# First message layer of a two-layer graph network: the steps of the last four chunks drawn together, with gathers up to three chunks ahead

## The chip, the cores and the metric

One core of one Trainium2 chip runs the whole kernel in one launch. The metric is the device time of an execution in microseconds (us); lower is better. The engines are PE (TensorE), DVE (VectorE), ACT (ScalarE), POOL (GpSimd, which here issues the indirect gathers) and SP (SyncE, which issues the plain DMAs).

## The reference

The graph has 12,500 nodes of 128 features and 400,000 edges, sorted by destination. Two layers are computed, each on the normalized and rectified nodes `h = relu(layernorm(x))`:

```
# layer 0, per edge:
h   = relu([h[src], h[dst], edge_attr] @ We1 + be1)      # 32 wide
em  = relu(h @ We2 + be2)                                # 128 wide
h2  = relu([h[dst], em] @ Wn1 + bn1)                     # 64 wide
nm  = relu(h2 @ Wn2 + bn2)                               # 128 wide
x  += h + segment_sum(nm, dst)
# layer 1, per edge, with 8 relations:
H   = einsum('ni,rio->rno', relu(layernorm(x)), W)
x  += relu(segment_sum((H[type, src] + b[type]) * weight, dst))
```

## The kernel before, in words

Layer 0 works on 391 chunks of 1,024 edges (`NC` = 391, `CT` = 8 tiles of 128 edges; the last chunk has the number L = 390). Three chunks make a span, whose destinations lie in one window of 128 nodes; there are 131 spans. One chunk passes through these steps, each a method of `Edges` (line numbers of the kernel before):

- `gathered` (L765, by `gather_a`, L426): eight indirect gathers issued by POOL (L394), two to one tile `gb`, which fetch the source's 32-wide product from `tab_a`.
- `turned` (L472): four DVE transposes of `gb` (L477) into `agT`. Each waits for its two gathers to land.
- `end_T` (L453, DVE): one-hot of the destinations for the window's products.
- `first` (L467, L469, PE into the bank `pre`), `first_src` (L485, DVE, twice, into `z`), `first_end` (L489, ACT).
- `second` (L496 PE into `pm0`, `pm1`; L501 ACT, twice).
- `third` (L507, L510 PE into `u`; L513 ACT).
- `fourth` (L520, PE into `pq0`, `pq1`), `fourth_sum` (L528 DVE and L529 ACT, twice each), `fourth_end` (L534 DVE, twice); the last two together are `valued`.
- `ends` (L539, DVE): one-hot `oh` of the destinations, two buffers.
- `sum_up` (L755, by `fifth`, L548 PE): eight matmuls that add the chunk into the span's bank `acc`; the span's last chunk also brings in the row carried from the span before (L554).

When a span is complete, `Span.end` (L749) and `rows_h` (L600) turn its 128 sums into rows of layer 1: a reduction of `acc` (L559), a normalization (L604, L579, L581, L583 on ACT, L588, L590), a transpose (L612 on PE, L614 on ACT), two products of 512 columns (L619) with their additions (L620), and a store into `tab_h` (L621). They are drawn in pieces, one at each `node_step`; `Span.deviate` and `Span.begin` prepare the window's own nodes (L579 to L583, and L588, L590, L596). The PSUM banks `pre`, `pm0`, `pm1`, `u`, `pq0`, `pq1` and `acc` exist once each.

The order of SP, DVE, ACT and PE is the order in which the program draws the instructions: `in_order` ties each to the one drawn before it on its engine. The loop at L801 is a software pipeline written by hand. Turn i draws `first` of chunk i, `second` and `third` of chunk i-1, `fourth` and `valued` of chunk i-2, `sum_up` of chunk i-3, the gathers of chunk i+1 and their four transposes, spread over the turn. So a chunk takes four turns, and three turns without a new chunk follow chunk L. In `gather_a`, `past` says which earlier chunk's transposes a gather must wait for ("not too far ahead"): near the end that is the chunk just before.

Layer 1 starts when all of `tab_h` is stored. Its POOL queue holds 3,128 gathers (L394 too, into `hg`), which DVE multiplies and reduces and PE adds up.

Of the kernel before, what the change touches and what calls it, by code (L numbers as in the profile page):

```python
# [31 lines left out]
CT = 8  # L32
CE = CT * P
SC = 3
ST = SC * CT
NT = -(-E // P)
NC = -(-E // CE)
NS = -(-NC // SC)
# [5 lines left out]
GT = 2  # L44
# [10 lines left out]
def gnn_kernel(  # L55
# [43 lines left out]
    def in_order(start, *engines):  # L99

        for i in block.bb.instructions[start:]:
            if i.engine in engines:
                if i.engine in queues:
                    tc.add_manual_dep(
                        i, queues[i.engine].name,
                        mybir.DependencyInfo(mybir.DependencyClass.NoSync,
                                             mybir.DependencyReason.DATA), reason="in order")
                queues[i.engine] = i
# [62 lines left out]
    def from_byte(table, first, n, most):  # L171

        row = in_bytes(table)
        width = row.shape[1]
        first = nc.s_assert_within(
            first, 0, most * width, skip_runtime_bounds_check_because="a least dst is a node")
        return row.rearrange("n d -> (n d)")[ds(first, n * width)].rearrange("(n d) -> n d", n=n)
# [12 lines left out]
    with tc.tile_pool(name="n0", bufs=2) as pool, \  # L190
# [18 lines left out]
        def products():  # L209

            i, q, m, hT = quads.pop(0)
            (acb, rs), (g, n) = acbs[i], groups[i]
            pn = psum.tile([P, 4, P], F32, name="pn")
            for j in range(m):
                nc.tensor.matmul(pn[:, j, :], hT[:, j, :], w_node, start=True, stop=True)
            if i > len(groups) // 2 and q % 8:
                nc.vector.tensor_copy(acb[:, q:q + m, :], pn[:, :m, :])
            else:
                nc.scalar.copy(acb[:, q:q + m, :], pn[:, :m, :])
            if q + m == n:  # L220
                at = pool.tile([P, GJ, 32], F32, name="at")
                nc.vector.tensor_tensor(at[:, :n, :], acb[:, :, 0:32],
                                        rs[:, :, None].to_broadcast([P, n, 32]), op=OP.mult)
                nc.sync.dma_start(a_g[:, g:g + n, :], at[:, :n, :])

        def turned(i):
            n = groups[i][1]
            for q in range(0, n, 4):
                m = min(4, n - q)
                pt = psum.tile([P, 4, P], F32, name="pt")  # L230
                for j in range(m):
                    nc.tensor.transpose(pt[:, j, :], xms[i][:, q + j, :], ident)
                hT = pool.tile([P, 4, P], F32, name="hT", bufs=4)
                nc.scalar.activation(hT[:, :m, :], pt[:, :m, :], AF.Relu)
                quads.append((i, q, m, hT))
                if len(quads) > 2:
                    products()

        for i, (xg, (g, n)) in enumerate(zip(xs, groups)):
# [4 lines left out]
            k = g - g0  # L244
# [25 lines left out]
            if i >= 3:  # L270
                turned(i - 3)
        for i in range(max(0, len(groups) - 3), len(groups)):
            turned(i)
# [150 lines left out]
    turns = {}  # L424

    def gather_a(idx, c=None):  # L426


        gbs = []
        past = c and c - max(1, 16 - c // 8)  # L430
        for t in range(0, CT, GT):
            gb = gpool.tile([P, GT, 32], F32, name="gb", bufs=16 * CT // GT)
            key = None if c is None else f"gb{c}_{t}"
            gather([gb[:, j, :] for j in range(GT)], tab_a, [idx(t + j) for j in range(GT)], key,
                   turns.get((past, t // GT)))
            gbs.append((gb, key))
        return gbs

    class Edges:
# [25 lines left out]
        def first(self, eat):  # L465
            self.pre = self.psum.tile([64, 512], F32, name="pre")
            nc.tensor.matmul(self.pre, w_ea, eat, start=True, stop=False)  # L467
            for h in range(2):
                nc.tensor.matmul(self.pre[32 * h:32 * h + 32, :], self.win[:, 64:96],  # L469
                                 self.half_T(h), start=False, stop=True)  # L470
# [66 lines left out]
        def ends(self, rel):  # L537
            self.oh = self.pool.tile([P, CT, P], F32R, name="oh", bufs=2)
            nc.vector.tensor_tensor(self.oh, self.iota[:, None, :].to_broadcast([P, CT, P]),  # L539
                                    rel[:, :, None].to_broadcast([P, CT, P]), op=OP.is_equal)  # L540
# [11 lines left out]
    def carry(acc, s, sums):  # L552

        nc.tensor.matmul(acc[0:1, 0:D], carried[:, s:s + 1], sums, start=False, stop=False)  # L554
# [69 lines left out]
    with tc.tile_pool(name="e0", bufs=2) as pool, \  # L624
# [6 lines left out]
        chunks, spans, rows, relbs, eats = {}, {}, {}, {}, {}  # L631
        active = []
        before = [None]

        def node_step():
            if active and next(active[0], "done") == "done":
                active.pop(0)
# [21 lines left out]
        def load(c):  # L659
            if c < NC:  # L660
                chunks[c] = Edges(pool, psum, iota_p, nid_p)
                chunks[c].load_win(from_byte(tab_cb, rows[c // SC][c % SC], WR, 3 * (NP - WB)))
# [92 lines left out]
        def sum_up(c):  # L755
            s, k = divmod(c, SC)
            of = spans[s]
            if k == 0:
                of.acc = psum.tile([P, 2 * D], F32, name="acc")
            stop = k == SC - 1 or c == NC - 1  # L760
            chunks.pop(c).fifth(of.acc, k == 0, stop,
                                (lambda: carry(of.acc, s, before[0])) if stop and s else None)
            return spans.pop(s) if stop else None

        def gathered(c):  # L765
            idx = src0 if c * CT < T0 else src_sb
            return gather_a(lambda t: idx[:, c * CT + t:c * CT + t + 1], c)
# [4 lines left out]
        def valued(c):  # L772
            chunks[c].fourth_sum()
            chunks[c].fourth_end()
# [4 lines left out]
        def end_T(c):  # L779
            chunks[c].ends_T(relbs[c // SC][:, c % SC, :])  # L780
# [12 lines left out]
        gbs = gathered(0)  # L793
# [4 lines left out]


        L = NC - 1  # L800
        for i in range(L + 3):  # L801
            s, k = divmod(i, SC)
            new, two, three = i <= L, 0 < i <= L + 1, 1 < i
            if i < L:
                gbs = gathered(i + 1)

            def turned(q):
                if i < L:
                    turns[i + 1, q] = chunks[i + 1].turned(q, gbs[q])

            if new:
                first(i)
            if k == SC - 1:
                load_eat(s + 2)
            if two:
                chunks[i - 1].second()
            whole = sum_up(i - 3) if i > 2 else None
            if new:
                chunks[i].first_src()
                chunks[i].first_end()  # L820
            turned(0)
            if three:
                chunks[i - 2].fourth()
                ends(i - 2)
            turned(1)
            if i < L:
                end_T(i + 1)
            if k == 1:
                head(s + 2)
                load_relb(s + 2)  # L830
            if k == 0:
                node_step()
            turned(2)
            if three:
                chunks[i - 2].fourth_sum()
            node_step()
            if two:
                chunks[i - 1].third()
            turned(3)
            if three:  # L840
                chunks[i - 2].fourth_end()
            load(i + AHEAD)
            if k == 0:
                if s:
                    spans[s - 1].begin()
                if s not in spans:
                    spans[s] = Span(s)
            if k == 1 and new:
                spans[s].deviate()
            if i == L - 2:  # L850
                for s in range(s + 1, NS):
                    spans[s] = Span(s)
            if i == L - 1:
                for s in range(s + 1, NS):
                    spans[s].deviate()
            if i == L + 1:
                spans[NS - 1].begin()
            if whole:
                active.append(whole.end(["pre"] * 3))
            next(prepared, None)  # L860


        last = sum_up(L)
        node_step()
        steps = last.end(("u", "pm0", "pm1"))
        for k in range(3):
            node_step()
            next(steps)
        for _ in steps:
            pass  # L870
        in_order(start, ENG.SP, ENG.DVE, ENG.Activation, ENG.PE)


# [281 lines left out]
```

## Time and profile before

| | us |
|---|---|
| median of 3 runs (lowest, highest) | 7961.75 (7959.56, 7962.12) |
| profiled execution, its own time | 7943.7 |
| its span in the profile | 7941.9 |
| POOL busy | 5946.7 (75%) |
| DVE busy | 5323.5 (67%) |
| PE busy | 3699.1 (47%) |
| first gather of layer 1 starts at | 4021.04 |

All moments in this document are microseconds from the start of the span. A line of the timeline gives the start, the duration, engine, line, operation, tiles and count, and in brackets the idle time of the engine before it and what ended that. A line of the table by stretches gives for each engine its busy time and, in parentheses, its instructions, then the granted clock of PE (1.00 is full), the DMA share and GB/s.

### The profile page before, as it was taken

Reading aid. Unit: us, or ns where it says so; the run is one execution under the profiler, and the core shown is the slowest. Engines: PE = TensorE matmul, PEld = TensorE weight load, DVE = VectorE, ACT = ScalarE, POOL = GpSimd, SP = SyncE. Lnnn points to the kernel's source line nnn. Section 1 sums busy time; section 2 is a strip of 40 time slices with the busy share of each in tenths; the row PEclk is TensorE's granted clock in tenths of the full one; section 3 lists DMA queues with packets and bytes.
Section 4 is the critical chain, followed back from the end, with each engine's and each line's share of the span. In section 5 each row is a group of like instructions: output and inputs, shape, how many; then the busy total and the mean of one; then the engine's idle time right before and its main releaser. Section 6 shows DMA issues by size and latency. Waiting matters only on the chain. (4 is left out here: it accounts for less than half of the span.)

```text
span 7941.9 us, 54373 instructions
## 1 busy us (share of the span) xinstructions
PE 3699.1 (47%) x13981; PEld 1867.5 (24%) x13982; DVE 5323.5 (67%) x9464; ACT 1691.9 (21%) x3217; POOL 5946.7 (75%) x6273
## 2 busy tenths in 40 slices
PE   4888888888888888888821111111111110111111
PEld 2444444444444444444410000000000000000000
DVE  7978777777777777777755555555555555555555
ACT  3433333333333333333310000000000000000000
POOL 6777777777777777777767777777777777777776
PEclk7988988888888888888855555555555555555555
DMA  5544433333333323333222222222222222222222
GB/s 167 146 99 97 99 91 87 94 87 90 91 88 92 91 87 94 88 90 91 87 56 57 57 57 57 57 57 57 57 57 57 57 57 57 57 57 57 57 57 54
DMA packets 605541, 614.39 MB, mean 77 GB/s; under 512 B 361633, under 2 KB 465893, under 8 KB 604767
## 3 DMA queue, kind: packets, MB, share of 16 engines
q1 hardware_dynamic: 403064, 353.77, 14.3%
q0 software_dynamic: 200192, 256.65, 14.3%
q8 instruction: 115, 1.88, 0.1%
q14 instruction: 206, 1.68, 0.1%
q10 hardware_dynamic: 1964, 0.41, 0.0%
HBM read 509.91 MB, written 100.43 MB: 77 GB/s over the span
## 5 line engine op out<-in xcount | busy, mean ns | idle before, releaser
L394 POOL DMA_INDIRECT hg<-tab_h,hidx_sb x3128 | 2951.3, 944 | 993.3 <-issue 952.6
L394 POOL DMA_INDIRECT gb<-tab_a,src_sb x3032 | 2863.9, 945 | 924.1 <-issue 722.6
L1070 DVE TENSOR_TENSOR v<-hg,io_p 128x1024 f32<-128x1024 f32 x782 | 960.0, 1228 | 1619.2 <-DMA hg<-tab_h,hidx_sb 1610.3
L1040 PE MATMUL acc<-hm,oh 128*128 128x256 f32 x782 | 347.5, 512 | 3514.6 <-DVE oh L1035 3481.5
L1040 PEld LDWEIGHTS acc<-hm,oh 128*128 128x128 f32 x782 | 205.7, 304 | 3675.3 <-issue 3640.4
L1075 DVE TENSOR_REDUCE sm<-v 128x128 f32<-128x1024 f32 x782 | 959.1, 1227 | 9.0
L1078 ACT CAST hm<-sm 128x256 fp32r<-128x256 f32 x391 | 145.5, 372 | 3778.0 <-DVE sm L1075 3778.0
L477 DVE STREAM_TRANSPOSE agT<-gb 128x64 f32<-128x64 f32 x1564 | 376.5, 241 | 734.0 <-DMA gb<-tab_a,src_sb 715.4
L520 PE MATMUL pq<-w_n,h 128*128 128x256 f32 x3128 | 846.7, 420 | 0.0
L529 ACT ACTIVATE nm<-pq 128x512 fp32r<-128x512 f32 x782 | 449.0, 597 | 1339.3 <-DVE pq L528 1338.2
L467 PE MATMUL pre<-eats,w_ea 128*64 128x512 f32 x782 | 473.8, 691 | 481.2 <-DVE ht L620 278.0
L520 PEld LDWEIGHTS pq<-w_n,h 128*128 128x128 f32 x3128 | 647.8, 217 | 89.5 <-issue 0.8
L548 PE MATMUL acc<-nm,oh 128*128 128x256 f32 x3128 | 607.0, 335 | 21.6 <-DVE nm L534 16.7
L548 PEld LDWEIGHTS acc<-nm,oh 128*128 128x128 f32 x3128 | 479.9, 221 | 434.8 <-issue 134.4
L501 ACT ACTIVATE em<-pm,b_e 128x512 f32<-128x512 f32 x782 | 491.0, 678 | 400.8 <-PE pm L496 400.2
L528 DVE TENSOR_TENSOR pq<-pq,b_n 128x512 f32<-128x512 f32 x782 | 505.1, 682 | 58.6 <-PE pq L520 55.9
L496 PE MATMUL pm<-h,w_e 32*128 32x512 f32 x1564 | 526.8, 755 | 0.0
L534 DVE SCALAR_TENSOR_TENSOR nm<-pq,nm 128x512 fp32r<-128x512 f32 x782 | 489.6, 664 | 0.1
L453 DVE TENSOR_TENSOR ohT<-relb,io_p 126x1024 bf16<-126x1024 bf16 x391 | 462.2, 1182 | 6.2 <-DMA relb<-rel_d 6.2
L539 DVE TENSOR_TENSOR oh<-io_p,rel_s 128x1024 fp32r<-128x1024 f32 x391 | 463.3, 1185 | 0.0
L510 PE MATMUL u<-em,w_msg 128*64 128x512 f32 x1564 | 419.8, 616 | 0.2 <-ACT em L501 0.2
L485 DVE TENSOR_TENSOR z<-pre,agT 64x256 f32<-64x256 f32 x782 | 317.3, 406 | 33.0 <-PE pre L469 23.0
(125 smaller groups left out, 3443.5 us busy)
## 6 DMA issues: line engine op xcount, KB each, us to landing
eats<-in_ea SPq DMA_DIRECT2D x131, 768.0 KB
relb<-rel_d SPq DMA_DIRECT2D x131, 756.0 KB
tab_h<-ht SPq DMA_DIRECT2D x131, 576.0 KB
hg<-tab_h,hidx_sb POOLq DMA_INDIRECT x3128
gb<-tab_a,src_sb POOLq DMA_INDIRECT x3032
win<-tab_cb SPq DMA_DIRECT2D x391, 23.6 KB
xw<-tab_h SPq DMA_DIRECT2D x131, 64.0 KB
out<-o SPq DMA_DIRECT2D x131, 64.0 KB
```

What stands on the lines that cost most here:

```text
L394: g = nc.gpsimd.indirect_dma_start(out=out, out_offset=None, in_=table, in_offset=bass.IndirectOffsetOnAxis(ap=idx, axis=0))
L467: nc.tensor.matmul(self.pre, w_ea, eat, start=True, stop=False)
L496: nc.tensor.matmul(pm, w_e2[rows, :], self.h1[rows, :], start=True, stop=True)
L501: nc.scalar.activation(em, pms[h], AF.Relu, bias=b_e2)
L520: nc.tensor.matmul(pq[:, 2 * i:2 * i + 2, :], self.h2[:, P * (2 * k + i):P * (2 * k + i) + P], w_n2, start=True, stop=True)
L528: nc.vector.tensor_add(pq, pq, b_n2[:, None, :].to_broadcast([P, 4, D]))
L534: nc.vector.scalar_tensor_tensor(nm[:, :, 1, :], pq, 0.0, nm[:, :, 0, :], op0=OP.max, op1=OP.subtract)
L539: nc.vector.tensor_tensor(self.oh, self.iota[:, None, :].to_broadcast([P, CT, P]), rel[:, :, None].to_broadcast([P, CT, P]), op=OP.is_equal)
L548: nc.tensor.matmul(acc, self.oh[:, i, :], self.nm[:, at, :, :].rearrange("p q d -> p (q d)"), start=(start and i == 0), stop=(stop and i = ...
L1040: nc.tensor.matmul(acc[:, 0:2 * D], oh[:, q, :], hm[:, q, :, :].rearrange("p r d -> p (r d)"), start=begin and q == 0, stop=stop and q == 1)
L1070: reads(nc.vector.tensor_tensor(v, hg, w_p[:, q, t:t + CT, None].to_broadcast([P, CT, D]), op=OP.mult), f"hg{c}")
L1075: nc.vector.tensor_reduce(sm[:, q, :], v.rearrange("p t d -> p d t"), AX.X, OP.add)
```

## The change

The loop now ends after turn L-4. The last four turns, and what follows, are written out. In them a chunk's steps no longer stand in four different turns: chunks L-4, L-3 and L-2 catch up, chunk L-1 has `first` to `valued` in its own turn, and chunk L too. The four transposes of chunks L-1 and L stand together at the end of the turn before. The instructions are the same ones, in the same number. For chunks above L-5 the gathers wait for the transposes of the chunk three before them.

```diff
-        past = c and c - max(1, 16 - c // 8)
+        past = c and c - (3 if c > NC - 6 else max(1, 16 - c // 8))
...
-        for i in range(L + 3):
+        for i in range(L - 3):
...
+        i = L - 3
+        gbs = gathered(i + 1)
+        first(i)
+        chunks[i - 1].second()
+        sum_up(i - 3)
+        begun(i)
+        turned(i + 1, 0)
+        chunks[i - 2].fourth()
+        ends(i - 2)
+        node_step()
+        turned(i + 1, 1)
+        end_T(i + 1)
+        node_step()
+        chunks[i - 1].third()
+        valued(i - 2)
+        load(L)
+        node_step()
+        spans[s - 2].begin()
+        spans[s - 1] = Span(s - 1)
+        ends(i - 1)
+        chunks[i - 1].fourth()
+        valued(i - 1)
+        node_step()
+        turned(i + 1, 2)
+        turned(i + 1, 3)
+
+        i = L - 2
+        gbs = gathered(i + 1)
+        first(i)
+        chunks[i - 1].second()
+        sum_up(i - 3)
+        whole = sum_up(i - 2)
+        begun(i)
+        ends(i - 1)
+        end_T(i + 1)
+        chunks[i - 1].third()
+        chunks[i].second()
+        chunks[i - 1].fourth()
+        close(whole)
+        chunks[i - 1].fourth_sum()
+        chunks[i].third()
+        chunks[i - 1].fourth_end()
+        node_step()
+        ends(i)
+        chunks[i].fourth()
+        valued(i)
+        spans[s - 1].deviate()
+        spans[s] = Span(s)
+        node_step()
+        all_turned(i + 1)
+
+        i = L - 1
+        gbs = gathered(L)
+        first(i)
+        sum_up(i - 2)
+        sum_up(i - 1)
+        begun(i)
+        node_step()
+        chunks[i].second()
+        end_T(L)
+        ends(i)
+        node_step()
+        chunks[i].third()
+        spans[s - 1].begin()
+        spans[s].deviate()
+        chunks[i].fourth()
+        valued(i)
+        spans[s].begin()
+        all_turned(L)
+
+        first(L)
+        whole = sum_up(L - 1)
+        begun(L)
+        close(whole)
+        chunks[L].second()
+        ends(L)
+        node_step()
+        chunks[L].third()
+        node_step()
+        chunks[L].fourth()
+        node_step()
+        valued(L)
+        node_step()
+        for _ in sum_up(L).end(("u", "pm0", "pm1")):
+            pass
```

Here `begun` is `first_src` and `first_end`, `all_turned` the four transposes, and `close` starts the rows of a complete span; `s` is L / 3 = 130.

More of the change, by code (lines that the diff above doesn't have):

```diff
@@ L800, in gnn_kernel, with turned, begun @@
         L = NC - 1
-        for i in range(L + 3):
-            s, k = divmod(i, SC)
[L803 to L812, printed above, removed]
+        def turned(c, q):
+            turns[c, q] = chunks[c].turned(q, gbs[q])
+        def begun(c):
+            chunks[c].first_src()
+            chunks[c].first_end()
+        for i in range(L - 3):
+            s, k = divmod(i, SC)
+            two, three = 0 < i, 1 < i
+            gbs = gathered(i + 1)
+            first(i)
             if k == SC - 1:
@@ L817, in gnn_kernel @@
             whole = sum_up(i - 3) if i > 2 else None
[L818 to L821, printed above, removed]
+            begun(i)
+            turned(i + 1, 0)
             if three:
@@ L824, in gnn_kernel @@
                 ends(i - 2)
-            turned(1)
-            if i < L:
-                end_T(i + 1)
+            turned(i + 1, 1)
+            end_T(i + 1)
             if k == 1:
@@ L832, in gnn_kernel @@
                 node_step()
-            turned(2)
+            turned(i + 1, 2)
             if three:
@@ L838, in gnn_kernel @@
                 chunks[i - 1].third()
-            turned(3)
+            turned(i + 1, 3)
             if three:
@@ L847, in gnn_kernel @@
                     spans[s] = Span(s)
-            if k == 1 and new:
+            if k == 1:
                 spans[s].deviate()
[L850 to L857, printed above, removed]
             if whole:
@@ L860, in gnn_kernel, with all_turned, close @@
             next(prepared, None)
-        last = sum_up(L)
-        node_step()
[L865 to L869, printed above, removed]
+        def all_turned(c):
+            for q in range(CT // GT):
+                turned(c, q)
+        def close(whole):
+            active.append(whole.end(["pre"] * 3))
+        assert L % SC == 0
+        s = L // SC
+        i = L - 3
+        gbs = gathered(i + 1)
@@ new lines, in gnn_kernel @@
+        first(i)
+        chunks[i - 1].second()
+        sum_up(i - 3)
+        begun(i)
+        turned(i + 1, 0)
+        chunks[i - 2].fourth()
+        ends(i - 2)
+        node_step()
+        turned(i + 1, 1)
+        end_T(i + 1)
[10 more added lines that the diff above has]
+        node_step()
@@ new lines, in gnn_kernel @@
+        turned(i + 1, 2)
+        turned(i + 1, 3)
+        i = L - 2
+        gbs = gathered(i + 1)
+        first(i)
[4 more added lines that the diff above has]
+        ends(i - 1)
+        end_T(i + 1)
+        chunks[i - 1].third()
[6 more added lines that the diff above has]
+        node_step()
@@ new lines, in gnn_kernel @@
+        ends(i)
[7 more added lines that the diff above has]
+        gbs = gathered(L)
+        first(i)
+        sum_up(i - 2)
+        sum_up(i - 1)
+        begun(i)
+        node_step()
[7 more added lines that the diff above has]
+        chunks[i].fourth()
@@ L870, in gnn_kernel @@
+        valued(i)
[15 more added lines that the diff above has]
+        for _ in sum_up(L).end(("u", "pm0", "pm1")):
             pass
+        assert not active and not spans
         in_order(start, ENG.SP, ENG.DVE, ENG.Activation, ENG.PE)
```

## The prediction

> **What bounds the kernel now.** I read the groups of the page first, then POOL's timeline, then DVE's over the end of layer 0, then the table by stretches for PE's clock.
>
> ```profile
> L394 POOL DMA_INDIRECT hg<-tab_h,hidx_sb x3128 | 2951.3, 944 | 993.3 <-issue 952.6
> L394 POOL DMA_INDIRECT gb<-tab_a,src_sb x3032 | 2863.9, 945 | 924.1 <-issue 722.6
> ```
>
> Both layers are paced by POOL's gathers: 944 ns and 0.30 us of issue, 1.25 us each, ten for a chunk. Layer 1's 3,128 gathers take 3,903 us whenever they start. So the change can act only on their start.
>
> ```profile
> 3979.78 0.94 POOL L394 DMA_INDIRECT gb<-tab_a,src_sb  x1 [0.31 <-issue]
> 4021.04 0.94 POOL L394 DMA_INDIRECT hg<-tab_h,hidx_sb  x1 [40.32 <-DVE io_p L1029]
> ```
>
> POOL stands still for 40.3 us between the layers: that is all there is to win. Every earlier gather in the last 55 us follows its forerunner by 0.30 us, so none waits for an older chunk's transposes.
>
> ```profile
> 3984.03 0.24 DVE L477 STREAM_TRANSPOSE agT<-gb 128x64 f32<-128x64 f32 x1 [1.28 <-DMA gb<-tab_a,src_sb]
> ...
> 4016.42 0.69 DVE L620 TENSOR_TENSOR ht<-pm,b_f 128x512 f32<-128x512 f32 x1 [1.02 <-PE pm L619]
> ...
> 4020.00 0.43 DVE L1025 TENSOR_TENSOR is<-rel_t 128x96 f32<-128x96 f32 x2 [2.47 <-DMA tab_h<-ht]
> ```
>
> The last gathers land at 3984.0; 33 us of steps of chunks 388 to 390 follow; the last store of `tab_h` lands at 4020.0, and 1.04 us later POOL starts. What counts is the time of that landing.
>
> ```profile
> 3958.62:3962.03 3.41, 1.51 (x8) 0.47 (x8) 2.02 (x6) 1.37 (x4) 2.77 (x3) 0.96 0.13 22
> 3962.03:3965.44 3.41, 3.41 (x6) 0.88 (x8) 2.96 (x8) 0.51 (x1) 2.52 (x3) 0.50 0.12 16
> ...
> 4002.99:4006.40 3.41, 1.92 (x11) 1.34 (x11) 2.82 (x9) 0.29 (x1) 0.00 (x0) 0.96 0.43 173
> 4006.40:4009.82 3.42, 2.02 (x3) 0.73 (x3) 1.50 (x6) 0.46 (x2) 0.00 (x0) 0.50 0.00 0
> ```
>
> After stretches in which PE was busy for about half (1.51 and 1.92 of 3.41 us) its granted clock is 0.50, both times for 10.2 us; a product L619 then takes 1.04 us in place of 0.51.
>
> **The change part by part.** *Wider distance of the gathers.* It removes nothing: no gather waits now. In the new order chunk 389's transposes come late (below), and chunk 390's gathers, from 3971.05 on, would have to wait for them; with distance three they wait for chunk 387's, done by 3954, so POOL still ends at 3980.7. Value: 0.
>
> *SP.* The same loads and stores. The load of `xt_last` moves behind a store of rows; it is wanted only some 25 us later, against 2.9 us that the last store takes (issued 4017.1, landed 4020.0). The last `win` is loaded in the turn in which it was before. Value: 0. If a load were late, some 3 us.
>
> *The order of DVE, ACT and PE.* No instruction is added or dropped. What changes is what each waits for. Before, neighbours in a queue belong to four chunks, so one chunk's latency is filled by another's work. Drawn together, a chunk's `second`, `third`, `fourth` and `valued` follow each other in the queues, and PE, ACT and DVE hand one chunk back and forth. I followed this chain through the new queues, from `ends` of chunk 385 (L539, at 3956.36 in the trace, up to which both orders are alike) to the landing of the last store. Spacings at full clock are from the rows of these 60 us: L477 0.17, L485 0.42, L528 0.60, L534 0.59, L539 and L453 1.11, L620 0.62 on DVE; L529 0.60, L513 and L489 0.7, L501 0.6 on ACT; on PE `first` 1.32, `second` 1.07 (both halves run at once and end together), `third` 1.28, `fourth` 1.80, `fifth` 1.09, L619 0.98, L554 0.30; 0.04 to 0.12 at each change of engine.
>
> - Turn 387, to the bank `pre` freed for chunk 388: 1.11 + 0.66 (L539, L588, L590), PE L612 and `third` 1.5, ACT 1.35, then DVE without a pause: L534 twice, L620, L588/L590/L596, L539, L528 twice, 0.6 of ACT, L534, L620 = 11.7 us. The gathers no longer matter here; PE stands idle for 3.5 us at the end of it, since `first` of 388 needs `pre`, which is freed by an L620 queued behind both `valued`.
> - Turn 388 on PE: `first` 1.4, `second` 1.1, two `fifth` and L554 2.4, `third` 1.3, `second` 1.1, `fourth` 1.8 = 9.1.
> - `valued` of 387 and 388, then L579, L581, L583, L614, before `pre` is free again: 0.8 + 0.6 + 0.7 + 0.5 + 1.2 + 1.3 + 0.6 + 0.7 + 0.5 + 0.5 = 7.4. PE has little to do in it.
> - Turn 389 on PE: `first` 1.32, two `fifth` 2.18, L619 0.98, `second` 1.07, L619 0.98, `third` 1.28 = 7.8 (the chain of waits runs through PE's order here).
> - L513 0.8, `fourth` 1.8, L528 0.8, L529 0.6, L534 0.7, L588/L590/L596 0.8 = 5.5. Only now come the four transposes of chunk 390, at about 3998 although their gathers landed at 3984.0. What they waited for, the DMA, is no longer late; DVE's own queue is.
> - The last chunk: transposes and `z` 1.6, L489 0.8, `second` 1.1, L501 1.3, L510 0.6, L513 0.7, `fourth` 1.9, then L619 1.0 and L620 0.7 of the span before, L528 1.3, L529 and L534 1.4, `fifth` and L554 1.4, L559 and L604 to L581 1.3, L583 to L590 0.9, L612 and L614 0.7, two L619 2.0, L620 0.8, store 3.0 = 22.5.
>
> Sum 64.0 us at full clock, against 63.6 in the trace (4020.0 - 3956.4), which holds two stretches at half clock. Followed in the same way with those two stretches, the old order gives 63.3, so the method is off by some 0.3 us.
>
> *Half clock in the new order.* PE is less than half busy in the 3.5 us of turn 387, in the 7.4 us of the third item and in much of the last 22 us. I count three stretches of half clock of 6.8 to 10.2 us. PE is on the chain for all of the first (6.8 holds 3.4 us of full-clock work: +3.4, at most +5.1), nearly all of the second (+3.1 to +4.6), a third of the last (+1.2 to +1.8): +7.7 to +11.5, I take +9.6. Ends: 0 if full clock is granted throughout, and +25 if all 27 us of PE work on the chain from 3968 run at half clock.
>
> [...]
>
> Total: 64.0 + 9.6 - 63.6 = +10 us. The profiled execution took 7943.7 us by its own time (span 7941.9), so its like is 7953.7; the median of the runs lies 18 us above that, and the same 10 us on it give 7972. A measurement of this kernel can tell about 0.2%, 16 us, from no change: this is within.
>
> **The rivals.**
>
> A. *Half clock stays to the end* (slower). If PE, fed one chunk at a time, never again fills the stretches that give the clock back (those before its returns at 3972 and 4016.6 were busy 3.41 and 3.15 of 3.41), all PE work from 3968 doubles: 64.0 + 25 - 63.6 = +26, 7988; from the second idle place on, +20. It is decided when half clock costs over 15.5 us, that is over some 17 us of PE work on the chain. For it: the new chain leaves PE idle in every item but two. Against: items two and four are 8 to 9 us of unbroken PE work. Chance 0.35, for +16 to +26.
>
> B. *The catching up works* (faster). If chunk 389 is through before 3984.0, only the last chunk's 22.5 us follow the landing: 4006.5, with 1.5 for half clock 4008, -12 us, 7950. To be faster by over 0.2% it would need 4004.1, full clock and 2 us less in that chain. Against it: 14.5 us of waits in the items would have to be absent, while DVE in the trace has only 1 to 3 us free in a turn. Chance 0.07, of it 0.03 beyond 0.2%.
>
> C. *Nothing moves.* Full clock nearly throughout, as the chain of 64.0 says by itself: +0.4, 7962. Chance 0.04.
>
> **How the numbers follow.** The forecast, +3 to +16, has 0.54. Slower is A: 0.35. Faster is 0.03 of B. Same is 0.54 + 0.04 + 0.04 = 0.62. The range runs from C (7961; B lies below it, 0.07) to 7984, +22 within A, with about 0.1 above.
>
> **What would show it.** Right, if POOL's last `gb` still starts near 3979.8; if the transposes of chunk 390 start near 4003 to 4007 with no DMA as their releaser; if PE waits some 3 us before `first` of 388 for L620 and before `first` of 389 for ACT's L614; if the clock is 0.50 after those places; and if the first `hg` starts near 4031. Wrong, if chunk 390's transposes are released by the DMA at 3984 (B), if the clock stays at 0.50 from 3968 on (A), or if a gather of chunk 390 waits for DVE. If the pace of layer 1 differs from 1.25 us a gather, my ground is wrong altogether.

## The result, and the profile after

The changed kernel took 7,970.59 us (median of 22 runs, 7,968.61 to 7,974.84), the kernel before 7,960.98 us in the same comparison (22 runs, 7,958.02 to 7,965.3): a ratio of 1.0013, 95% interval 1.0007 to 1.0019, or +9.6 us. That is inside the 0.2% which the prediction called the same, and +10 us had been forecast. The profiled execution took 7,968.61 us by its own time (span 7,966.8).

That execution is 24.9 us longer than the profiled one of before, not 9.6. The groups of its profile say why:

```profile
L394 POOL DMA_INDIRECT hg<-tab_h,hidx_sb x3128 | 2958.1, 946 | 1003.0 <-issue 953.1
L394 POOL DMA_INDIRECT gb<-tab_a,src_sb x3032 | 2871.2, 947 | 924.6 <-issue 725.8
```

A gather took 946 and 947 ns where it took 944 and 945 ns: the two groups are busy 14.1 us longer, spread evenly over both layers. The medians of the runs differ by 9.6 us only; the profiled execution of before lay 18 us below the median of its kernel, this one 2 us below. What can be compared between two profiled executions is therefore not a moment but the time POOL stands idle between the layers, in which no gather runs. POOL's timeline of the changed kernel (the last gather of layer 0, the first of layer 1, idle time in brackets):

```profile
3987.86 0.94 POOL L394 DMA_INDIRECT gb<-tab_a,src_sb  x1 [0.30 <-issue]
4038.38 0.94 POOL L394 DMA_INDIRECT hg<-tab_h,hidx_sb  x1 [49.58 <-DVE io_p L1107]
```

49.58 us in place of 40.32: +9.3 us, nearly the whole of the difference of the medians. Below, "the gap" is this number, and every run is read by it. It comes from one profile of each kernel; the old order has two (the kernel before and f4_distance), which are 0.5 us apart.

The two places where the prediction saw PE run dry, in PE's timeline (`first` of 388 and of 389):

```profile
3975.61 1.65 PE L467 MATMUL pre<-eats,w_ea 128*64 128x512 f32 x2 [3.47 <-DVE ht L620]
...
3995.20 1.07 PE L467 MATMUL pre<-eats,w_ea 128*64 128x512 f32 x2 [3.14 <-ACT hT L614]
```

PE waits 3.47 us for L620 and 3.14 us for L614, the two releasers that the prediction named. DVE's timeline of the end:

```profile
4010.07 0.62 DVE L477 STREAM_TRANSPOSE agT<-gb 128x64 f32<-128x64 f32 x4
...
4020.56 0.69 DVE L620 TENSOR_TENSOR ht<-pre,b_f 128x512 f32<-128x512 f32 x1 [6.16 <-PE pre L619]
...
4037.33 0.43 DVE L1103 TENSOR_TENSOR is<-rel_t 128x96 f32<-128x96 f32 x2 [2.48 <-DMA tab_h<-ht]
```

Chunk 390's transposes start without any releaser, 22 us after the last of their gathers was issued: the DMA is not late any more, DVE's own queue is. Near the end DVE sits idle 6.16 us for a product, and the last store lands at 4037.33. In this trace PE's granted clock changes only at moments that lie whole multiples of 3.41 us apart (3975.96, 3982.79, 3996.44, 3999.85 and so on). A piece of that length is called a window below, and one or more windows in a row at 0.50 a stretch of half clock. The table by stretches, cut at these windows (length; busy time and count of PE, PEld (PE's loading of weights), DVE, ACT, POOL; PE's granted clock; DMA share; GB/s):

```profile
3972.55:3975.96 3.41, 0.35 (x1) 0.19 (x2) 3.16 (x7) 1.13 (x2) 2.51 (x3) 1.00 0.11 19
3975.96:3979.38 3.42, 3.42 (x8) 0.61 (x6) 0.83 (x2) 0.00 (x0) 2.51 (x4) 0.50 0.61 201
...
3992.99:3996.44 3.45, 1.24 (x4) 0.29 (x4) 2.14 (x8) 0.92 (x3) 0.00 (x0) 1.00 0.01 2
3996.44:3999.85 3.41, 3.41 (x17) 3.31 (x16) 0.83 (x2) 0.72 (x1) 0.00 (x0) 0.50 0.00 0
...
4010.09:4013.51 3.42, 2.01 (x12) 0.69 (x10) 3.20 (x12) 1.02 (x2) 0.00 (x0) 1.00 0.00 0
4013.51:4016.92 3.41, 3.21 (x9) 0.80 (x7) 0.85 (x3) 1.27 (x2) 0.00 (x0) 0.50 0.00 0
...
4020.33:4023.75 3.42, 1.70 (x4) 0.48 (x3) 3.05 (x5) 1.17 (x2) 0.00 (x0) 1.00 0.00 0
4023.75:4027.16 3.41, 2.67 (x9) 1.73 (x9) 1.21 (x4) 0.00 (x0) 0.00 (x0) 0.50 0.43 173
```

PE did 0.35, 1.24, 2.01 and 1.70 us of work in these windows at full clock, and each time the next window had the clock at 0.50. In all there were four stretches of half clock, from 3975.96, 3996.44, 4013.51 and 4023.75, of 6.8, 3.4, 3.4 and 10.2 us.

### The profile page after: what moved, and what is told of

It is laid out like the page before. It is cut to its first block, busy times and chain, and to the rows that moved or that the text cites. A ratio compares the mean times of both kernels' runs of the same rounds, so it can differ in the third digit from the quotient of the medians.

```text
span 7966.8 us, 54372 instructions
## 1 busy us (share of the span) xinstructions
PE 3713.5 (47%) x13981; PEld 1874.9 (24%) x13982; DVE 5322.0 (67%) x9464; ACT 1693.7 (21%) x3217; POOL 5960.0 (75%) x6273
## 5 line engine op out<-in xcount | busy, mean ns | idle before, releaser
L520 PE MATMUL pq<-w_n,h 128*128 128x256 f32 x3128 | 850.4, 421 | 3.1 <-ACT h L513 2.1
L520 PEld LDWEIGHTS pq<-w_n,h 128*128 128x128 f32 x3128 | 648.9, 218 | 96.9 <-ACT h L513 4.8
L496 PE MATMUL pm<-h,w_e 32*128 32x512 f32 x1564 | 527.4, 756 | 1.4 <-ACT h L489 1.4
L539 DVE TENSOR_TENSOR oh<-io_p,rel_s 128x1024 fp32r<-128x1024 f32 x391 | 463.4, 1185 | 3.2 <-PE acc L548 3.2
```

What stands on the lines that cost most here:

```text
L496: nc.tensor.matmul(pm, w_e2[rows, :], self.h1[rows, :], start=True, stop=True)
L520: nc.tensor.matmul(pq[:, 2 * i:2 * i + 2, :], self.h2[:, P * (2 * k + i):P * (2 * k + i) + P], w_n2, start=True, stop=True)
```

## The experiments

Theory: the loss is a little longer chain at full clock and, for the greater part, half clock on that chain. Rivals: the distance of the gathers; the serial waits alone, with the clock of no account; the late start of the last chunk. The 95% intervals of the ratios below are some 7 us wide to each side, as large as most effects, so that the gap says more than the time.

**Four runs whose times could not tell.** They met a chip on which the kernel before took 9,474.22 us.

```
e1_distance: the old order of the last turns, and only
+        past = c and c - (3 if c > NC - 6 else max(1, 16 - c // 8))
e2_order: the changed kernel with the old line
+        past = c and c - max(1, 16 - c // 8)
e3_warm: the changed kernel, and
+        io_p = psum.tile([P, 3 * P], F32, name="io_p")
+        warm = io_p[:, 2 * P:3 * P]
+        def keep(n):
+            for _ in range(n):
+                nc.tensor.matmul(warm, ident, ident, start=True, stop=True)
...
+        keep(9)                    # ahead of first(L - 2)
+        keep(9)                    # ahead of first(L - 1)
+        keep(5)                    # ahead of chunks[L].second()
+        keep(2)                    # ahead of chunks[L].third()
+        keep(5); keep(8)           # around sum_up(L).end(...)
e4_moves: the changed kernel, and
         node_step()                # turn 387, behind valued(L - 5) and load(L)
+        node_step()                # ahead of spans[s - 2].begin(), ends(L - 4), valued(L - 4)
...
-        node_step()                # not behind valued(L - 4)
+        first(L - 1)               # turn 388: ahead of valued(L - 2), not at the head of turn 389
```

> The old order of the last turns with the new distance of three chunks alone. The measure is the idle time of POOL between the last gather of layer 0 and the first of layer 1 (40.3 us before, 49.6 after), since the pace of the gathers differs by some 10 to 20 us from one profiled execution to another. My theory (the drawn-together chain with its half clock makes the loss; the distance does nothing in the old order, since no gather waited there): the gap stays at 40 to 41 us, and the time is that of the kernel before within 3 us. Rival (the distance changes when gathers start or how fast they run, and the loss is there): the gap goes to about 49 us, or the time rises by some 9 us with the gap unchanged.

> The new order of the last turns with the old distance. My theory: chunk 390's gathers now have to wait for chunk 389's transposes, so the last gather starts some 15 us later (about 4003 in place of 3988) but lands just before its transposes, which start at about 4010 for reasons of their own; the time is then that of the changed kernel within 3 us (7967 to 7974), and the gap of POOL falls to some 32 to 36 us only because its left end moves. The rival that the wider distance cost the time: back to the time of the kernel before, 7961.

> The changed kernel, with 38 extra products of 128x128 in the last four turns, placed where PE stood idle, into columns of the bank io_p that nothing reads. They change no wait but fill PE's windows. My theory (0.4 us of the loss is the chain, 9.6 us half clock): the granted clock shows 1.00 almost throughout from 3970 on, the gap of POOL falls from 49.6 to 40 to 42 us, and the time comes back to that of the kernel before within 2 us (7959 to 7964). Rival (the loss is the waits of a chain in which one chunk's steps follow each other, and the clock matters little): the gap stays at 48 to 50 us or grows by what the extra products delay.

> The changed kernel with two steps moved and nothing else: one node_step in turn 387 ahead of both valued and of ends (so that the bank pre is free for first of 388 before PE runs dry), and first of 389 ahead of valued of 387 in turn 388 (so that PE has it while DVE and ACT work on both valued). Both named waits of PE (3.5 us before first of 388, 3.1 us before first of 389) should then be gone or short. My theory: the two idle places also cause two of the stretches at half clock, so the gap falls by more than the waits themselves, from 49.6 to some 38 to 45 us, and the time to 7957 to 7966. Rival (the waits are slack, and DVE's queue sets the end): the gap stays at 48 to 50 us.

Measured against that 9,474.22: 9,486.29, 9,483.24, 9,490.98 and 9,497.42 us, ratios 1.0012 (1.0003 to 1.0021), 1.0011 (1.0002 to 1.002), 1.0018 (1.0009 to 1.0027) and 1.0031 (1.002 to 1.0043). On the face of it everything made it slower, the change's parts and their opposites alike. The groups of e1_distance show that the ground is another one:

```profile
L394 POOL DMA_INDIRECT gb<-tab_a,src_sb x3032 | 2870.0, 947 | 1993.9 <-DVE agT L477 1179.5
L394 POOL DMA_INDIRECT hg<-tab_h,hidx_sb x3128 | 3292.6, 1053 | 1118.1 <-issue 1060.6
```

POOL waits 1,994 us in layer 0, mostly for the transposes, where it had waited 924 us, mostly for its own issue; and a gather of layer 1 takes 1,053 ns in the mean. Layer 0 is no longer paced by gathers there, so the last turns meet another state of the queues. Why shows only in part: in the timeline of e1_distance, PE's record of the products L520 ends at 3074.5, yet DVE's next instruction, which needs them, starts 7 us later, by a release that no recorded engine gave:

```profile
3081.83 1.30 DVE L528 TENSOR_TENSOR pq<-pq,b_n 128x512 f32<-128x512 f32 x2 [8.07 <-remote]
```

What held it is open. The same four kernels were run again on chips on which the kernel before took its usual time; the comparisons rest on those. (The last two chunks of e2_order and e3_warm ran free of such waits and are used further below.) The kernel before took 7,946 to 7,961 us on these chips, so each run is compared with the kernel before on its own chip.

**f1_warm: e3_warm again, PE kept busy.**

> The same kernel as e3_warm (the changed kernel with 38 extra products of 128x128 where PE stood idle, into columns of io_p that nothing reads), run again, because the first four runs met a chip on which even the kernel before took 9,474 us in place of 7,961: there layer 0 lasted to 5,056 us and its gathers waited for the transposes, so that they can't tell the theories apart. Asked of a run in which the kernel before takes some 7,961 us. My theory (0.4 us of the loss is the chain, 9.6 us half clock): clock 1.00 almost throughout from 3970 on, gap of POOL between the layers 40 to 42 us, time that of the kernel before within 2 us. Rival (serial waits; the clock matters little): the gap stays at 48 to 50 us or more.

7,949.82 us against 7,949.10: ratio 1.0001 (0.9992 to 1.0010), +0.7 us. From its timelines of POOL and DVE and the table by stretches:

```profile
4025.24 0.94 POOL L394 DMA_INDIRECT hg<-tab_h,hidx_sb  x1 [42.19 <-DVE io_p L1119]
```

```profile
4000.85 0.62 DVE L477 STREAM_TRANSPOSE agT<-gb 128x64 f32<-128x64 f32 x4
```

```profile
3967.49:3970.91 3.42, 2.27 (x18) 2.08 (x18) 3.29 (x7) 1.13 (x2) 2.51 (x4) 1.00 0.22 34
3984.56:3987.97 3.41, 2.28 (x18) 1.76 (x17) 2.69 (x9) 1.59 (x4) 0.00 (x0) 1.00 0.10 5
4005.04:4008.45 3.41, 2.89 (x15) 1.61 (x15) 0.14 (x1) 1.46 (x4) 0.00 (x0) 1.00 0.00 0
```

The stretches in which PE had run dry now hold 2.27 to 2.89 us of work, the clock is 1.00 up to the last store, and the gap falls from 49.58 to 42.19 us although 38 instructions were added to the chain's engine. The order of the kernel's own steps was not touched, and the long waits stay (`first` of 388 starts 11.63 us after `ends` of 385 in both kernels); only the products themselves wait twice for L539, with which they share `io_p` (0.26 and 0.43 us). `second` of chunk 387 (L496) takes 1.13 us where it took 2.08 at half clock. The expectation (gap 40 to 42, time within 2 us of before) holds to 0.2 us; the rival, for which the clock was of no account, falls.

**f2_moves: e4_moves again, the two idle places taken away.**

> The same kernel as e4_moves (the changed kernel with one node_step in turn 387 drawn ahead of both valued and ends, and first of 389 drawn ahead of valued of 387 in turn 388), for a chip on which the kernel before takes some 7,950 to 7,961 us. My theory, after f1_warm showed a gap of POOL of 42.2 us with the clock kept at 1.00: PE's waits of 3.5 and 3.1 us are gone or short, and with them one or two of the four stretches at half clock; gap 38 to 46 us, time between that of the kernel before and 4 us above it. Rival (the idle places of PE cost no more than their own length, or are slack): the gap stays at 47 to 50 us, the time 8 to 10 us above.

7,950.42 us against 7,946.52: ratio 1.0006 (0.9997 to 1.0015), +3.9 us. Timelines of PE (`first` of 388 and 389) and POOL:

```profile
3967.89 1.07 PE L467 MATMUL pre<-eats,w_ea 128*64 128x512 f32 x2
...
3981.26 1.07 PE L467 MATMUL pre<-eats,w_ea 128*64 128x512 f32 x2
```

```profile
4026.06 0.94 POOL L394 DMA_INDIRECT hg<-tab_h,hidx_sb  x1 [42.78 <-DVE io_p L1107]
```

(The node_step goes ahead of `ends` and of one `valued`, that of 386; "both" in the expectation is one too many. And `first` of 389 goes ahead of `valued` of 388, not of 387.) Neither `first` waits now, the first two stretches at half clock are gone (the only ones left start at 4001.34 and 4011.58, in the last chunk), and the gap falls by 6.8 us: inside the 38 to 46 us and the 0 to 4 us expected. Two steps drawn elsewhere give back most of the gap that the change cost. By itself this run does not part the half clock from the waits, which were 6.6 us together; f1_warm does.

**f3_order: e2_order again, the old distance.**

> The same kernel as e2_order (the new order with the old distance of the gathers). My theory: the last gather starts some 12 to 17 us later (chunk 390's wait for chunk 389's transposes), lands just before its own transposes, and the time is that of the changed kernel within 3 us (7 to 13 us above the kernel before). If the gathers then come later than their transposes would have, up to 5 us more. Rival (the wider distance is what costs): the time of the kernel before.

7,958.73 us against 7,946.52: ratio 1.0014 (1.0005 to 1.0023), +12.2 us, as expected (7 to 13). Timelines of POOL and DVE:

```profile
3992.22 0.94 POOL L394 DMA_INDIRECT gb<-tab_a,src_sb  x1 [15.28 <-DVE agT L477]
...
4036.10 0.94 POOL L394 DMA_INDIRECT hg<-tab_h,hidx_sb  x1 [34.18 <-DVE io_p L1107]
```

```profile
4006.48 0.24 DVE L477 STREAM_TRANSPOSE agT<-gb 128x64 f32<-128x64 f32 x1 [0.22 <-DMA gb<-tab_a,src_sb]
```

Chunk 390's gathers wait 15.28 us for a transpose of chunk 389, and land so late that the last of their four transposes waits 0.22 us for them. From `ends` of 385 to the landing of the last store this kernel took 75.0 us, the changed one 73.35. So the wider distance is worth at most some 2 us in the new order, and taking it away does not bring the loss back.

**f4_distance: e1_distance again, the distance alone.**

> The same kernel as e1_distance (the old order with the new distance of the gathers alone), for a chip on which the kernel before takes some 7,950 to 7,961 us. My theory: no gather waited in the old order, so the gap of POOL is 40 to 41 us and the time that of the kernel before within 2 us. Rival: the distance itself costs, with a gap of 45 us or more, or a time 5 us or more above the kernel before.

7,955.82 us against 7,956.17: ratio 1.0000 (0.9991 to 1.0009).

```profile
4028.48 0.94 POOL L394 DMA_INDIRECT hg<-tab_h,hidx_sb  x1 [39.79 <-DVE is L1025]
```

The gap is 39.79 us, just under the 40 to 41 expected: in the old order the distance does nothing that the gap shows. With f3_order this settles that the order of the steps holds the loss.

**e5_turns: the last chunk's transposes early.**

```
 begun(i)                   # turn 389
+all_turned(L)
 node_step()
...
-all_turned(L)              # not behind valued(L - 1)
```

> The changed kernel with the four transposes of chunk 390 drawn early, just after begun of 389 in turn 389 in place of after valued of 389. They then start near 3991 in place of 4010 (on the times of the changed kernel's profile). My theory: they are 0.6 us of DVE's time and nothing waits for them before first of 390, whose place on PE is behind third of 389; the gap of POOL falls by 0 to 3 us, from 49.6 to 47 to 49.6, and the time stays 7 to 10 us above the kernel before. Rival (that the last chunk starts late is what costs): the gap falls by 8 us or more, to 41 us.

7,957.84 us against 7,946.52: ratio 1.0012 (1.0003 to 1.0021).

```profile
3992.21 0.62 DVE L477 STREAM_TRANSPOSE agT<-gb 128x64 f32<-128x64 f32 x4
```

```profile
4029.81 0.94 POOL L394 DMA_INDIRECT hg<-tab_h,hidx_sb  x1 [47.56 <-DVE io_p L1107]
```

The transposes start some 11 us earlier against their gathers than in the changed kernel, and the gap falls by only 2.0 us, as expected; the rival falls. The reason is not quite the expected one, the place on PE. `first` of 390 is over at 4003.1, and `first_src` follows at 4004.56, when DVE has come through `valued` of 389 and L588 to L596: what the last chunk waits for is its place in DVE's queue. Counted from `first` of 389, `first_src` starts only 0.7 us earlier than in the changed kernel (14.89 against 15.59). Since this profile has also 13.7 us of half clock in place of 23.9, not even the 2.0 us can be put down to the transposes. The time does not follow the gap here (+11.3 us where 7 to 10 were expected); its 11 runs lie over 9 us, and the profiled one was among the faster, so the 2 us cannot be told from nothing by the time.

**e7_two: only the first two groups of extra products.** It is f1_warm without the last four `keep`.

> The changed kernel with only the first two groups of extra products (nine of 128x128 ahead of first of 388 and nine ahead of first of 389), none in the last chunk. It splits the half clock's part of the loss. My theory, by the terms of the prediction (first two stretches 3.4 to 5.1 and 3.1 to 4.6 us, the last 1.2 to 1.8): the gap of POOL falls from 49.6 to 42 to 45.5 us and the time to 2 to 5 us above the kernel before. Rival (the last chunk's stretches hold most of the loss): the gap stays at 46.5 us or more.

7,961.76 us against 7,956.17: ratio 1.0007 (0.9998 to 1.0016), +5.6 us. Timeline of POOL, and the stretches about 4010:

```profile
4034.81 0.94 POOL L394 DMA_INDIRECT hg<-tab_h,hidx_sb  x1 [46.68 <-DVE io_p L1115]
```

```profile
4006.89:4010.30 3.41, 1.81 (x7) 0.60 (x8) 2.98 (x8) 2.10 (x4) 0.00 (x0) 1.00 0.00 0
4010.30:4013.71 3.41, 3.04 (x6) 0.90 (x5) 0.00 (x0) 1.04 (x3) 0.00 (x0) 0.50 0.00 0
```

A miss: gap 46.68 us, where I expected 42 to 45.5 and the rival (the last chunk's stretches hold most of the loss) 46.5 or more, which it meets here. The first two stretches are gone, but in the last chunk a window with 1.81 us of work still takes the clock away for 6.8 us, and a second such stretch starts at 4023.95. Up to chunk 390's transposes its chain has the spacings of f1_warm to 0.01 us (11.63, 16.49 and 13.40); the last chunk takes 28.08 us in place of 23.35. The extra products of the last chunk alone were worth 4.5 us by the gap, and 4.9 by the times (f1_warm's +0.7 against +5.6, on two chips), not 1.2 to 1.8. In the changed kernel itself the last chunk holds 3.9 of 8.5 us of half clock (table further below).

**e8_oldwarm: the old order with PE kept busy.**

```
 (the old order, its last turns written out)
+ keep(2), keep(3), keep(10), keep(5), keep(3), ...    # 45 products at 14 places from turn 387 to the end
```

> The kernel before (old order, old distance), its last turns written out, with 45 extra products of 128x128 into columns of io_p that nothing reads, placed by following the chain so that PE's windows stay filled. It asks what half clock cost in the old order, whose two stretches the prediction left inside the 63.6 us that it subtracted. If the old order lost 2 to 3.5 us to them, the gap of POOL falls from 40.3 to 36.8 to 38.3 us, the time lies 2 to 3.5 us below the kernel before, and the new order's chain is, clock for clock, longer by some 3 us and not by 0.4. Rival (those stretches lay off the old chain, which was bound by the gathers' landing at 3984): the gap stays at 39.8 to 40.8 us and the time within 1 us.

7,943.00 us against 7,946.01: ratio 0.9996 (0.9987 to 1.0005), -3.0 us. Timelines of POOL and DVE:

```profile
4021.36 0.94 POOL L394 DMA_INDIRECT hg<-tab_h,hidx_sb  x1 [38.57 <-DVE io_p L1131]
```

```profile
3981.81 1.22 DVE L539 TENSOR_TENSOR oh<-io_p,rel_s 128x1024 fp32r<-128x1024 f32 x1 [2.67 <-PE io_p L638]
```

The clock is 1.00 from 3952.0 to 4020.3, the landing. The gap is 38.57 us, a little above the 36.8 to 38.3 expected, and the time is within the 2 to 3.5 us expected. So half clock probably did cost the old order something: 1.75 us by the gap against the profile of before, 1.2 against that of f4_distance (the old order too). More can't be read, since the extra products, which lie in the tile `io_p`, made L539 wait for them (2.67 us here). The gap speaks against the rival (nothing lost to half clock), by two to three times the 0.5 us between the two profiles of the old order; by the time alone the interval still holds 1.

**e6_order: a third order, and a version that beats both.**

```
 (from chunk 389's second on)
 chunks[L - 1].second()
 end_T(L)
 sum_up(L - 3)
 node_step()
 turned(L, 1)
 spans[s - 1].begin()
 turned(L, 2)
 chunks[L - 1].third()
 first(L)
 spans[s].deviate()
 turned(L, 3)
 chunks[L - 1].fourth()
 sum_up(L - 2)
 begun(L)
 node_step()
 chunks[L - 1].fourth_sum()
 chunks[L].second()
 ends(L - 1)
 chunks[L - 1].fourth_end()
...
```

> The same steps of the last four turns in a third order, looked for by following the chain through the queues with the durations of the traces and the clock's behaviour in them: steps of three or four chunks interleaved as before, so that PE always has another chunk's work, but each chunk's steps as early as its gathers allow, first of a chunk ahead of the older chunks' valued, all of chunk 389's steps up to third done before chunk 390's gathers land, and only the last chunk's 24 us behind that landing. The distance of the gathers stays three. My theory: the clock stays at 1.00 to the last chunk, the gap of POOL falls to 29 to 34 us (40.3 before, 49.6 after), and the time is 6 to 11 us below the kernel before. Rival (drawing a chunk's steps early cannot gain, since DVE's own work of the last 45 us sets the end): the gap stays at 39 us or more.

7,944.12 us against 7,956.17: ratio 0.9985 (0.9976 to 0.9994), -12.05 us. Timelines of POOL and DVE:

```profile
4016.59 0.94 POOL L394 DMA_INDIRECT hg<-tab_h,hidx_sb  x1 [30.01 <-DVE io_p L1112]
```

```profile
3990.13 0.24 DVE L477 STREAM_TRANSPOSE agT<-gb 128x64 f32<-128x64 f32 x1 [0.57 <-DMA gb<-tab_a,src_sb]
```

The gap is 30.01 us (29 to 34 expected; the time fell 1 us more than the 6 to 11), and the last of chunk 390's four transposes has the DMA as its releaser again: of the older chunks only 389's `valued`, the sums and the rows of their spans are left behind that landing, and they lie beside the last chunk's steps. This is the effect that rival B of the prediction priced at -12 us, by another order (-12.05 by the time, -10.3 by the gap). From 3946.9 to the last chunk the clock stays at 1.00 (the next window at half clock starts at 4008.4).

## Why the prediction was right, point by point

The chain can be cut at the same four moments in the changed kernel, in f1_warm, which is the same order at full clock, and in the prediction (us; L539 is that of chunk 385, "landing" that of the last store):

| from, to | changed | f1_warm | predicted at full clock |
|---|---|---|---|
| L539, `first` of 388 | 11.63 | 11.63 | 11.7 |
| to `first` of 389 | 19.59 | 16.49 | 9.1 + 7.4 = 16.5 |
| to the transposes of 390 | 14.87 | 13.40 | 7.8 + 5.5 = 13.3 |
| to the landing | 27.26 | 23.35 | 22.5 |
| sum | 73.35 | 64.87 | 64.0 |

The new order stands in six profiles, two of them from the first four runs. Some have extra products or the old distance, and they hold different amounts of half clock. From `first` of 388 to the landing (us):

| profile | half clock in it | length |
|---|---|---|
| f1_warm | 0 | 53.24 |
| e3_warm | 0 | 53.25 |
| e7_two | 13.7 | 57.97 |
| e2_order | 17.1 | 59.12 |
| changed | 23.9 | 61.72 |
| f3_order | 26.0 | 63.16 |

Against f1_warm each us at half clock goes with 0.34 to 0.38 us more, on the chips of these six profiles. This shows the cause better than the times do.

- **The chain at full clock** was 64.0 and is 64.9, the items each within 0.1 us but the last. Every spacing had been taken from a row and followed through the order of the queues, not through the busy shares.
- **Half clock on it** was +9.6 (7.7 to 11.5) and is 73.35 - 64.87 = 8.5. The sum was nearly right and its division wrong: it was to be 3.4, some 3.9 and some 1.5 us, with the rest for longer stretches; it was 3.1, 1.5 and 3.9. The second stretch lasted one window, not two or three. Why is open: that window was full (3.41 of 3.41 us, nearly all of it the two `fifth`), but so was the first window of the first stretch (3.42), and the clock stayed at 0.50 after it. The last chunk had two stretches, 13.7 us together, not one, and PE, which I put on the chain for a third of it, is on it for more. This is the mis-sized term, and e7_two is where it showed. That the second and the last item miss by -2.4 and +2.4 us, and the sums of half clock and full clock by -1.1 and +0.9, so that 73.35 meets the forecast 73.6, is luck.
- **The value before that was subtracted.** The prediction called the chain 0.4 us longer, 64.0 against 63.6. That was right as a sum and misleading as a cause, since the 63.6 held the old order's half clock. Clock for clock, f1_warm against e8_oldwarm: gaps of 42.19 and 38.57, so 3.6 us (by the times 0.7 + 3.0 = 3.7, on two chips). Of the +9.3 us of the gap some 3.6 are then the drawn-together chain, and 7.39 - 1.75 = 5.6 are more half clock. Counted from L539 of 385 in place of the last gather, it is 64.87 - 60.58 = 4.3 and 8.48 - 3.06 = 5.4. The two counts differ because that L539 does not stand at a fixed distance from the last gather (23.9 us ahead of it in the changed kernel, 22.8 in f1_warm), and in e8_oldwarm it waited 0.9 us for an extra product. So each share is good to about 1 us, with the reserve that extra products cost something themselves.
- **The distance, the loads: 0.** f4_distance and f3_order bear out the first. No load of SP shows as a releaser on the chain.
- **The marks.** The last `gb` was to start near 3979.8 and the first `hg` near 4031; they are 3987.86 and 4038.38, later by 8.1 and 7.4 us; 7.3 us of that are the longer gathers of layer 0 in that execution. Counted from the last `gb`, the first `hg` was to come 51.2 us later and comes 50.5 later. Chunk 390's transposes, 22.2 us after the last `gb`, are 1 to 5 us ahead of the mark for them, which fits the short second stretch. No gather of chunk 390 waited for DVE (0.30 us of issue before each). "Its like is 7953.7" was wrong by 15 us for the same reason: one profiled execution is no measure for another where 6,160 gathers can each be 2 ns slower.
- **The rivals.** A (half clock to the end) was wrong: 23.9 us in four stretches, with the clock back in between, after windows with 3.15 to 3.41 us of PE work. Its price was also some 2 us short: all of 27 us at half clock adds 27, not 25, since a product took 1.04 us in place of 0.51. B (the catching up works) did not come with this order; e6_order bears out its price with another order. C was not seen.
- **A window without a long gap.** The changed kernel's window from 4010.09 had 2.01 us of work in small pieces, with no gap of PE of more than 1.41 us, and the next one had the clock at 0.50 all the same. The four stretches of half clock in its end last 6.8, 3.4, 3.4 and 10.2 us, one to three windows.

What stays open: why a stretch lasts one window here and three there, since no run controlled that; and the chip of the first four runs.

## What to carry to other kernels

At this pipeline's end, drawing one chunk's steps together shortened nothing by itself: it moved waits from the DMA to the engines' own queues, and it emptied PE's windows, which cost more (some 5.5 us) than the longer chain (some 4). In the traces of the kernel before and of the changed one, from 3,700 to 4,040 us, no window of 3.41 us at full clock with 2.03 us of PE work or more was followed by one at 0.50. Where a trace shows the clock fall behind a window with less, put another chunk's work there (the gap of 49.58 us became 42.78 in f2_moves, 30.01 in e6_order), or products that nobody reads (42.19 in f1_warm), though not into a tile that another engine reads (e8_oldwarm: L539 waited 2.67 us for them). And price the end from the last input's landing: e6_order won by leaving as little as possible behind it. When the effect is 0.1%, read it from the one idle gap that it changes, not from two profiled spans.

## What the runs showed of the hardware that I had not expected

- The work in a window did not settle alone whether the next one had full clock. In the traces of the kernel before and of the changed one, from 3,700 to 4,040 us, 146 windows have full clock. After the 115 with 2.03 us of PE work or more in 3.41 the next window never had 0.50; after the 21 with 1.70 or less it had in 20, and after the 10 in between in 3. Kept, for example, after 1.41 us (the kernel before, from 3746.73), 1.53 (f3_order, from 3987.69) and 2.02 (e7_two, from 4017.13); lost after 1.81 (e7_two, from 4006.89) and 2.01 (the changed kernel, from 4010.09). In a window that was at half clock already, even 3.42 us did not always bring it back for the next (the changed kernel, from 3975.96).
- Extra products cost little: with 38 of 128x128 the chain was 64.87 us, 0.9 more than the sum predicted without them.
- One chip, used once, ran the same kernel 19% slower, with POOL waiting 1,994 us in layer 0 where it had waited 924. Four edits, among them one that does nothing elsewhere (f4_distance), all read as slower there.
